# Float16 parts in the experts' products, their weights' norms summed in the first stage, and sigmoids taken for two routing batches at once

## The chip, the cores and the metric

The kernel runs on one core of one Trainium2 chip. The core has five engines with instruction queues of their own: TensorE (PE in the profile; its weight loads are shown apart, as PEld), VectorE (DVE), ScalarE (ACT), GpSimd (POOL) and SyncE (SP, which here only issues DMAs). Each engine works through its queue in order, and semaphores tie the queues together. The metric is the time of one execution on the device, in microseconds (us). Several runs give a median; one further execution is recorded by the profiler, and its times are those of the profile.

## The reference

The input x is 4 sequences of 2048 tokens with 256 channels, 8192 tokens in all. It is normalised over the channels, and two branches are added to it:

```
xn = layernorm(x)
# branch 1: gated linear attention, 8 heads, keys of 128, values of 64
q, k, v = xn @ Wq, xn @ Wk * 128**-0.5, xn @ Wv
alpha = sigmoid((xn @ Wg + bg) / 16)
state[t] = alpha[t] * state[t-1] + outer(k[t], v[t])
attn = (q[t] @ state[t]) * sigmoid(xn @ Wog) @ Wo
# branch 2: mixture of 64 experts, 8 for each token
scores = sigmoid(xn @ gate_w.T)                 # 64 for each token
# groups of 8 experts, the best 4 groups, the best 8 experts in them,
# weights normalised and times 2.5; at most 256 tokens for an expert
y = (silu(rows @ w_gate[e]) * (rows @ w_up[e])) @ w_down[e]
out = x + attn + sum over its experts of weight * y
```

w_gate and w_up are 256x128 for each expert and w_down is 128x256, in float32: 393 KB for an expert and 25.2 MB for all 64.

## The kernel before

**Precision.** Most products are taken from two parts: a value is rounded to a high part, the rest is the low part, and `product` (L267) sums three matmuls: high times high, high times low, low times high. In the attention branch the parts are float16. Since float16 has a small range, a weight is first scaled by a power of two. The power comes from the weight's sum of squares, which ScalarE takes with a Square activation that also accumulates (`squares`, L153), or which TensorE takes (`gram`); two matmuls with the triangular matrices u_le and u_gt add the 128 partitions, and `fit_scales` (L159) makes the power out of the exponent's bits. In the experts' products the parts are of the type float32r, which has float32's range and needs no scaling.

**The attention branch** goes in 32 blocks of 256 tokens (`block`, L1034), and each block in 12 steps. A block projects keys, queries, gates and values (`project`, L810; its matmuls have the lines L269 to L271 and the tile pj). ScalarE takes the high part out of the accumulator and VectorE the low part (`split`, L219: lines L220 and L221, tiles k, qh, ql). The projections share four accumulator banks in the first half of the kernel; a bank is free when both engines have read it.

**The routing** goes in 16 batches of 512 tokens beside the attention of the first 16 blocks. It consists of generators in the list `side`: `front` (L333) normalises a batch and computes its logits, `decays` (L424) makes the decay factors of one to four batches, `back` (L481) selects the experts. Each call of `step()` moves each generator on by one `yield`, from the step number on that stands beside it in `side`. A batch's two sigmoids stand at the end of `front`: sg (L418), for the decays, and sc (L420), for the scores. ScalarE holds the tables of one set of functions; where the next function is not in it, the program has an ACT_TABLE_LOAD. The sigmoid is in another set than the exponential of the attention (L907), and the logarithm of `decays` (L432) in another again.

**The experts** begin with block 16, when `side` is empty: about five for each block, each in five stages at successive turns (`expert_step`, L722). `expert_weights` (L634) loads the three weights into w. `expert_in` (L641) turns the gathered rows (tile xet), and ScalarE takes the high parts wh (L653) and those of the rows (L655); VectorE takes the low part wl one turn later, in `expert_late` (L716, line L719). `expert_mid` (L659) has 12 matmuls into gu, a tanh (L668) and two operations of VectorE that give hs (L669, L671); `expert_split` makes hs into the parts hh and hl. `expert_out` (L681) has six matmuls into yp, and ScalarE multiplies by the routing weight (L691). `expert_add` (L702) adds the rows into the output by an indirect DMA of GpSimd.

**The order of the work.** The program's text gives the dependences, the pools' buffers and some pairs that must follow each other (`tc.issue_after`). A scheduler that simulates the engines then decides how the instructions stand in each engine's queue, and can draw work forward that comes later in the text. The order of the built program can be read without running it. The DMAs of SP stand in one queue, loads for the attention among those for the routing: xs (the block's rows), el, aj and mv (its decays), xt (the next batch), xw_d and xT_d (stores of a batch).

Of the kernel before, what the change touches and what calls it, by code (L numbers as in the profile page):

```python
# [8 lines left out]
F32 = mybir.dt.float32  # L9
F32R = mybir.dt.float32r  # L10
F16 = mybir.dt.float16
# [8 lines left out]
P = 128  # L20
# [25 lines left out]
KFIT = 2.0 ** -11  # L46
VFIT = 2.0 ** -14
FULL = 1024.0
NPART = 3
# [22 lines left out]
def gla_moe_kernel(ctx: ExitStack, tc: tile.TileContext, x, Wq, Wk, Wv, Wo, Wg, bg, Wog,  # L72
# [77 lines left out]
    unfit = const.tile([P, 6], F32, name="unfit")  # L150
    undo = const.tile([P, 1], F32, name="undo")

    def squares(j, t):  # L153
# [125 lines left out]
    r1 = routing.enter_context(tc.tile_pool(name="r1", bufs=1))  # L279
    stg = routing.enter_context(tc.tile_pool(name="stg", bufs=1))  # L280
    stg1 = routing.enter_context(tc.tile_pool(name="stg1", bufs=1))

# [50 lines left out]
    def front(b):  # L333
# [77 lines left out]
        for t in range(RT):  # L411
            for c in range(2):
# [4 lines left out]
                                       op0=ALU.mult, op1=ALU.add)  # L417
        nc.scalar.activation(sg[:, b], zs[:, b], AF.Sigmoid)  # L418
        sc = r3.tile([P, RT, E], F32, name="sc")
        nc.scalar.activation(sc, lg[:, :, 0:E], AF.Sigmoid, scale=unfit[:, GATE:GATE + 1])  # L420
        batch[b]["sc"] = sc
        yield True

# [57 lines left out]
    def back(b):  # L481
# [92 lines left out]
        yield True  # L574

    def lists():
# [56 lines left out]

    def expert_weights(e, m):  # L634
        w = moe["w4"].tile([P, 6, I], F32, name="w", bufs=3)
# [3 lines left out]
        m["w"] = w  # L639

    def expert_in(e, m):  # L641
# [8 lines left out]
        w3, m1 = moe["w3"], moe["m1"]  # L650
        wh = w3.tile([P, 6, I], F32R, name="wh")
        wl = w3.tile([P, 6, I], F32R, name="wl")
        nc.scalar.copy(wh, m["w"])  # L653
        x2 = m1.tile([P, 2, 2, 2, P], F32R, name="xe2")
        nc.scalar.copy(x2, xt)  # L655
        m.update(wh=wh, wl=wl, xh=x2[:, 0], xl=x2[:, 1])
        moe["late"].append((nc.vector, wl, m["w"], wh))

    def expert_mid(e, m):  # L659
# [3 lines left out]
        for k in range(2):  # L663
            for c in range(2):
                product(gu[:, k, :], (wh[:, 2 * k + c, :], wl[:, 2 * k + c, :]),
                        (xh[:, c], xl[:, c]), c == 0, c == 1)
        hs = moe["m1"].tile([P, CAP], F32, name="hs")
        nc.scalar.activation(hs, gu[:, 0, :], AF.Tanh, scale=0.5 / XFIT)  # L668
        nc.vector.scalar_tensor_tensor(hs, in0=hs, scalar=1.0, in1=gu[:, 0, :],  # L669
                                       op0=ALU.add, op1=ALU.mult)  # L670
        nc.vector.tensor_tensor(hs, hs, gu[:, 1, :], ALU.mult)  # L671
        m["hs"] = hs

    def expert_split(e, m):
        hh = moe["m2"].tile([P, CAP], F32R, name="hh")
        hl = moe["m2"].tile([P, CAP], F32R, name="hl")
        nc.scalar.copy(hh, m["hs"])
        moe["late"].append((nc.vector, hl, m["hs"], hh))
        m["h"] = (hh, hl)

    def expert_out(e, m):  # L681
# [8 lines left out]
        for f in range(2):  # L690
            nc.scalar.activation(y[:, f, :], yp[:, f, :], AF.Copy, scale=m["xe"][:, f, D + e:D + e + 1])  # L691
        m["y"] = y
# [23 lines left out]
    def expert_late():  # L716

        for eng, lo, full, hi in moe["late"]:
            eng.tensor_tensor(lo, full, hi, ALU.subtract)  # L719
        moe["late"] = []  # L720
# [481 lines left out]
    def start_front(b):  # L1202
        return 0 if b < 2 else 6 if b == 2 else (b - 2) * STEPS

    for b in range(NB):
        if b:
# [63 lines left out]
```

## Time and profile before

Three runs took 1246.44, 1246.57 and 1249.08 us.

| | us | share of the span |
|---|---|---|
| median of the runs | 1246.57 | |
| profiled execution | 1247.5 | |
| its span, first to last instruction | 1245.6 | 100% |
| TensorE busy | 1191.6 | 96% |
| weight loads busy | 1039.2 | 83% |
| VectorE busy | 967.7 | 78% |
| ScalarE busy | 858.6 | 69% |
| GpSimd busy | 710.5 | 57% |
| ScalarE's table loads, 39 of 1.283 each | 50.0 | 4% |

How to read it: a busy time is a union over the engine's instructions. Matmuls overlap each other and their weight loads, so the duration of one (some 0.28 us) is longer than the distance from one to the next, and the distance is what a matmul costs where TensorE is full. Instructions are grouped as "line engine operation out<-in shape xcount | busy us, mean ns | idle time of the engine just before, and what ended it". The kernel has three stretches: to about 60 us it sets up, to about 590 us the routing runs beside the attention, and from there to about 1195 us the experts do.

### The profile page before, as it was taken

What the parts mean: (1) busy time and instruction counts of PE and PEld (TensorE: products, weight loads), DVE (VectorE), ACT (ScalarE), POOL (GpSimd) and SP (SyncE); (2) the same over time, 40 slices, a digit from 0 to 9 for tenths busy, and PEclk for the clock granted to TensorE, in tenths of its full rate; (3) what the DMA queues carried; (4) which work ended last, traced back from release to release, by engine and by line L of the source; (5) the groups of instructions that cost most, each with busy time, mean ns of one, the idle gap of its engine ahead of it and who ended that gap; (6) DMA issues with size and microseconds to landing.
All of it is one profiled execution on the core that took longest, in us unless ns stands there. A gap on an engine that the chain in (4) does not pass through costs nothing.

```text
span 1245.6 us, 34787 instructions
## 1 busy us (share of the span) xinstructions
PE 1191.6 (96%) x13783; PEld 1039.2 (83%) x13783; DVE 967.7 (78%) x2669; ACT 858.6 (69%) x1536; POOL 710.5 (57%) x899
## 2 busy tenths in 40 slices
PE   6799999989999999999999999999999999999997
PEld 5587788878788788878789899998988898998986
DVE  6987787776777867777978878787878788787764
ACT  5566676666666566665667777777777777777764
POOL 1476577765676576753426665636856567665330
PEclk9999999999999999999999999999999999999999
DMA  7444444333344443322636675767767677766531
GB/s 245 126 129 153 113 130 126 121 96 110 94 128 119 136 128 104 101 67 75 186 101 143 161 174 127 171 149 176 155 157 168 155 160 170 161 143 147 104 68 35
DMA packets 148579, 165.35 MB, mean 133 GB/s; under 512 B 32384, under 2 KB 119296, under 8 KB 147712
## 3 DMA queue, kind: packets, MB, share of 16 engines
q1 hardware_dynamic: 114896, 113.57, 29.4%
q0 software_dynamic: 29712, 45.89, 21.4%
q10 hardware_dynamic: 3808, 3.67, 0.8%
q8 instruction: 108, 1.77, 0.6%
q14 instruction: 55, 0.45, 0.1%
HBM read 115.98 MB, written 58.38 MB: 140 GB/s over the span
## 4 chain that ended last, share of the span: by engine, by line
PE 67%; DVE 14%; ACT 8%; DMA 4%; POOL 4%; issue 2%; SPq 1%; DVEq 0%; ACTq 0%; POOLq 0%
PE pj L269 11%; PE pj L271 11%; PE pj L270 11%; PE od L948 4%; PE od L954 3%; PE kp L887 3%; DMA el<-el_d 3%; PE gu L269 2%; PE gu L271 2%; PE gu L270 2%; PE xet L649 2%; PE sp L269 2%; PE sp L270 2%; PE sp L271 2%; DVE qt L863 2%
## 5 line engine op out<-in xcount | busy, mean ns | idle before, releaser
L705 POOL DMA_INDIRECT out_dram<-y,idx x128 | 212.4, 1659 | 93.4 <-DMA out_dram<-y,idx 24.2
L629 POOL DMA_INDIRECT xe<-xw_d,idx x128 | 133.9, 1046 | 125.9 <-ACT y L691 85.8
L269 PE MATMUL pj<-xs,wq_h 128*128 128x256 f16 x496 | 135.4, 273 | 9.3 <-DVE k L221 8.2
L221 DVE SCALAR_TENSOR_TENSOR k<-pj,k 128x512 f16<-128x512 f32 x128 | 86.9, 685 | 70.4 <-ACT k L220 70.4
L269 PE MATMUL pj<-xs,wk_h 128*128 128x256 f16 x496 | 135.2, 273 | 0.1
L270 PE MATMUL pj<-xs,wq_h 128*128 128x256 f16 x496 | 135.2, 273 | 0.0
L271 PE MATMUL pj<-xs,wk_l 128*128 128x256 f16 x496 | 135.2, 273 | 0.0
L270 PE MATMUL pj<-xs,wk_h 128*128 128x256 f16 x496 | 135.2, 273 | 0.0
L271 PE MATMUL pj<-xs,wq_l 128*128 128x256 f16 x496 | 135.2, 273 | 0.0
L932 DVE TENSOR_TENSOR dc<-sp,dc 128x512 f32<-128x512 f32 x128 | 87.8, 686 | 40.4 <-PE sp L271 26.1
L948 PE MATMUL od<-dc,v 128*64 128x128 f32 x1024 | 102.5, 281 | 6.6 <-DVE dc L932 6.6
L220 ACT ACTIVATE k<-pj 128x512 f16<-128x512 f32 x128 | 74.8, 592 | 43.6 <-PE pj L271 43.2
L270 PE MATMUL sp<-ql,k 128*128 128x128 f16 x512 | 96.1, 219 | 4.2 <-DVE ql L221 3.9
L269 PE MATMUL sp<-qh,k 128*128 128x128 f16 x512 | 99.1, 220 | 0.9 <-ACT qh L220 0.8
L220 ACT ACTIVATE qh<-pj 128x512 f16<-128x512 f32 x128 | 75.9, 596 | 33.0 <-PE pj L271 32.2
L221 DVE SCALAR_TENSOR_TENSOR ql<-pj,qh 128x512 f16<-128x512 f32 x128 | 86.8, 679 | 11.9 <-ACT qh L220 11.7
L271 PE MATMUL sp<-qh,k 128*128 128x128 f16 x512 | 95.9, 219 | 0.0
L954 PE MATMUL od<-qt,state 128*64 128x128 f32 x960 | 94.5, 274 | 0.0
L719 DVE TENSOR_TENSOR wl<-w,wh 128x768 fp32r<-128x768 f32 x64 | 61.2, 956 | 40.5 <-ACT wh L653 37.9
L992 ACT CAST oh<-oT 128x512 fp32r<-128x512 f32 x64 | 39.5, 617 | 74.0 <-DVE oT L962 74.0
L863 DVE SCALAR_TENSOR_TENSOR qt<-pj,el 128x512 f32<-128x512 f32 x128 | 86.9, 679 | 0.0
L906 ACT ACTIVATE dc<-lp 128x512 f32<-128x512 f32 x128 | 76.2, 596 | 13.2 <-PE lp L902 13.2
(408 smaller groups left out, 4539.6 us busy)
## 6 DMA issues: line engine op xcount, KB each, us to landing
el<-el_d SPq DMA_DIRECT2D x64, 512.0 KB
xw_d<-x SPq DMA_DIRECT2D x16, 512.0 KB
xT_d<-xT SPq DMA_DIRECT2D x16, 512.0 KB
out_dram<-in_L_attn_x_dram SPq DMA_DIRECT2D x16, 512.0 KB
w<-in_L_ffn_w_gate_dram SPq DMA_DIRECT2D x64, 128.0 KB
w<-in_L_ffn_w_up_dram SPq DMA_DIRECT2D x64, 128.0 KB
w<-in_L_ffn_w_down_dram SPq DMA_DIRECT2D x64, 128.0 KB
xs<-xT_d SPq DMA_DIRECT2D x31, 256.0 KB
```

Source lines behind the costliest of these rows:

```text
L220: return (nc.scalar.activation(hi, t, AF.Copy, scale=scale).ins, nc.vector.scalar_tensor_tensor(lo, in0=t, scalar=scale, in1=hi, op0=ALU.m ...
L221: nc.vector.scalar_tensor_tensor(lo, in0=t, scalar=scale, in1=hi, op0=ALU.mult, op1=ALU.subtract).ins)
L269: nc.tensor.matmul(out_, lhsT=a[0], rhs=b[0], start=first, stop=False)
L270: nc.tensor.matmul(out_, lhsT=a[0], rhs=b[1], start=False, stop=False)
L271: return nc.tensor.matmul(out_, lhsT=a[1], rhs=b[0], start=False, stop=last).ins
L629: in_turn(lambda: nc.gpsimd.indirect_dma_start(out=xe[:, f, :], out_offset=None, in_=xw_d[:, :], in_offset=bass.IndirectOffsetOnAxis(ap=id ...
L705: two = [in_turn(lambda: nc.gpsimd.indirect_dma_start(out=of, out_offset=bass.IndirectOffsetOnAxis(ap=idx[:, e, f:f + 1], axis=0), in_=m[" ...
L863: read = nc.vector.scalar_tensor_tensor(qt, in0=pj, scalar=QFIT, in1=two_heads(el, i), op0=ALU.mult, op1=ALU.mult)
L906: nc.scalar.activation(dc, lp, AF.Relu, scale=-1.0)
L932: anchor.append(nc.vector.tensor_tensor(dc, B["sp"], dc, ALU.mult).ins)
L948: mm = nc.tensor.matmul(od[i * DV:(i + 1) * DV, n, j, :], lhsT=v[:, h0 + 2 * j + i, :], rhs=dc[:, 2 * j + i, :], start=True, stop=first)
L954: mm = nc.tensor.matmul(od[i * DV:(i + 1) * DV, n, j, :], lhsT=state[half][:, 2 * j + i, :], rhs=qt[:, ck, 2 * j + i, :], start=False, sto ...
```

## The change

Four things are altered.

1. **Types.** wh, wl, the rows' parts, hh and hl become float16. wh is now w times a power of two of the expert's own (`fite`), by an activation with a scale for each partition; wl, and hl likewise, come from a VectorE operation that scales, too. The tanh has the inverse as its scale (`arge`), the product that gives hs is scaled by 2^-44, and the routing weight of an expert's rows is multiplied by what is left over (`rese`), in a new small VectorE operation (`yw`, 128x2).
2. **Norms.** A new generator, `expert_fits`, joins `side` at step 16. It loads each expert's weights into one of three buffers nw and takes the sum of squares with one Square activation over 128x768; after the 64th, two matmuls add the partitions and five VectorE operations make the three scales of all experts. It yields two or three times after each expert.
3. **Loading.** The three DMAs of `expert_weights` move into `load_expert`, which both use. The experts' own loads remain.
4. **Sigmoids.** From batch 2 on, an even batch only has its logits copied into sc by VectorE. The odd batch after it takes sg of both batches in one activation, then the even batch's sc in place, then its own, one behind another.

```diff
+    sqe = const.tile([P, E], F32, name="sqe")
+    fite = const.tile([P, E], F32, name="fite")
+    arge = const.tile([P, E], F32, name="arge")
+    rese = const.tile([P, E], F32, name="rese")
...
+    nw = routing.enter_context(tc.tile_pool(name="nw", bufs=3))
...
-        nc.scalar.activation(sg[:, b], zs[:, b], AF.Sigmoid)
+
         sc = r3.tile([P, RT, E], F32, name="sc")
-        nc.scalar.activation(sc, lg[:, :, 0:E], AF.Sigmoid, scale=unfit[:, GATE:GATE + 1])
         batch[b]["sc"] = sc
+        if b > 1 and b % 2 == 0:
+            nc.vector.tensor_copy(sc, lg[:, :, 0:E])
+        else:
+            b0 = b if b < 2 else b - 1
+            made["sg"] = nc.scalar.activation(sg[:, b0:b + 1].rearrange("p b x y -> p (b x y)"),
+                                              zs[:, b0:b + 1].rearrange("p b x y -> p (b x y)"), AF.Sigmoid).ins
+
+            if b0 < b:
+                with tc.issue_after(made["sg"]):
+                    sc0 = batch[b0]["sc"]
+                    made["sg"] = nc.scalar.activation(sc0, sc0, AF.Sigmoid, scale=unfit[:, GATE:GATE + 1]).ins
+            with tc.issue_after(made["sg"]):
+                nc.scalar.activation(sc, lg[:, :, 0:E], AF.Sigmoid, scale=unfit[:, GATE:GATE + 1])
...
+    def expert_fits():
+
+        last = None
+        for e in range(E + 1):
+            if e < E:
+                w = nw.tile([P, 6, I], F32, name="nw")
+                load_expert(e, w)
+            if last is not None:
+                junk = stg1.tile([P, 6 * I], BF16, tag="junk", name="junk")
+                nc.scalar.activation(junk, last.rearrange("p c i -> p (c i)"), AF.Square,
+                                     accum_out=sqe[:, e - 1:e])
+            last = w
+            for _ in range(2 + e % 2):
+                yield True
+        tot = ps["mo"].tile([P, E], F32, tag="mo", name="tot")
+        for k, u in enumerate((u_le, u_gt)):
+            nc.tensor.matmul(tot, lhsT=u, rhs=sqe, start=(k == 0), stop=(k == 1))
...
-        wh = w3.tile([P, 6, I], F32R, name="wh")
-        wl = w3.tile([P, 6, I], F32R, name="wl")
-        nc.scalar.copy(wh, m["w"])
-        x2 = m1.tile([P, 2, 2, 2, P], F32R, name="xe2")
+        wh = w3.tile([P, 6, I], F16, name="wh")
+        wl = w3.tile([P, 6, I], F16, name="wl")
+        fe = fite[:, e:e + 1]
+        nc.scalar.activation(wh, m["w"], AF.Copy, scale=fe)
+        x2 = m1.tile([P, 2, 2, 2, P], F16, name="xe2")
...
-        nc.scalar.activation(hs, gu[:, 0, :], AF.Tanh, scale=0.5 / XFIT)
+        nc.scalar.activation(hs, gu[:, 0, :], AF.Tanh, scale=arge[:, e:e + 1])
...
-        nc.vector.tensor_tensor(hs, hs, gu[:, 1, :], ALU.mult)
+        nc.vector.scalar_tensor_tensor(hs, in0=hs, scalar=HFIT, in1=gu[:, 1, :], op0=ALU.mult, op1=ALU.mult)
         m["hs"] = hs
+        yw = moe["m2"].tile([P, 2], F32, name="yw")
+        nc.vector.tensor_scalar(yw, m["xe"][:, :, D + e], rese[:, e:e + 1], None, ALU.mult)
...
-            nc.scalar.activation(y[:, f, :], yp[:, f, :], AF.Copy, scale=m["xe"][:, f, D + e:D + e + 1])
+            nc.scalar.activation(y[:, f, :], yp[:, f, :], AF.Copy, scale=m["yw"][:, f:f + 1])
...
-            eng.tensor_tensor(lo, full, hi, ALU.subtract)
+            nc.vector.scalar_tensor_tensor(lo, in0=full, scalar=scale, in1=hi, op0=ALU.mult, op1=ALU.subtract)
...
+    side.append((16, expert_fits()))
```

More of the change, by code (lines that the diff above doesn't have):

```diff
@@ L47 @@
 VFIT = 2.0 ** -14
+HFIT = 2.0 ** -44
 FULL = 1024.0
@@ L574, in back @@
         yield True
+    def expert_fits():
[14 more added lines that the diff above has]
+            nc.tensor.matmul(tot, lhsT=u, rhs=sqe, start=(k == 0), stop=(k == 1))
+        y = stg1.tile([P, E], I32, tag="ye", name="ye")
+        nc.vector.tensor_copy(sqe, tot)
+        nc.vector.tensor_scalar(y, sqe.bitcast(I32), 24, None, ALU.logical_shift_right)
+        nc.vector.tensor_scalar(fite.bitcast(I32), y, -2.0 ** 23, 204 * 2.0 ** 23, ALU.mult, ALU.add)
+        nc.vector.tensor_scalar(arge.bitcast(I32), y, 2.0 ** 23, 39 * 2.0 ** 23, ALU.mult, ALU.add)
+        nc.vector.tensor_scalar(y, y, 20.0, 104.0, ALU.max, ALU.min)
+        nc.vector.tensor_scalar(rese.bitcast(I32), y, 3 * 2.0 ** 23, -60 * 2.0 ** 23, ALU.mult, ALU.add)
+        yield True
     def lists():
@@ L632, in fetch, with load_expert @@
         return dict(xe=xe)
-    def expert_weights(e, m):
-        w = moe["w4"].tile([P, 6, I], F32, name="w", bufs=3)
+    def load_expert(e, w):
         nc.sync.dma_start(out=w[:, 0:2], in_=w_gate[e].rearrange("(c p) i -> p c i", p=P))
@@ L638, in expert_weights @@
         made["w"] = nc.sync.dma_start(out=w[:, 4:6].rearrange("p c i -> p (c i)"), in_=w_down[e]).ins
-        m["w"] = w
+    def expert_weights(e, m):
+        m["w"] = moe["w4"].tile([P, 6, I], F32, name="w", bufs=3)
+        load_expert(e, m["w"])
     def expert_in(e, m):
@@ L650, in expert_in @@
         w3, m1 = moe["w3"], moe["m1"]
-        wh = w3.tile([P, 6, I], F32R, name="wh")
-        wl = w3.tile([P, 6, I], F32R, name="wl")
-        nc.scalar.copy(wh, m["w"])
-        x2 = m1.tile([P, 2, 2, 2, P], F32R, name="xe2")
+        wh = w3.tile([P, 6, I], F16, name="wh")
[3 more added lines that the diff above has]
+        x2 = m1.tile([P, 2, 2, 2, P], F16, name="xe2")
         nc.scalar.copy(x2, xt)
         m.update(wh=wh, wl=wl, xh=x2[:, 0], xl=x2[:, 1])
-        moe["late"].append((nc.vector, wl, m["w"], wh))
+        moe["late"].append((wl, m["w"], fe, wh))
     def expert_mid(e, m):
@@ L667, in expert_mid @@
         hs = moe["m1"].tile([P, CAP], F32, name="hs")
-        nc.scalar.activation(hs, gu[:, 0, :], AF.Tanh, scale=0.5 / XFIT)
+        nc.scalar.activation(hs, gu[:, 0, :], AF.Tanh, scale=arge[:, e:e + 1])
         nc.vector.scalar_tensor_tensor(hs, in0=hs, scalar=1.0, in1=gu[:, 0, :],
                                        op0=ALU.add, op1=ALU.mult)
-        nc.vector.tensor_tensor(hs, hs, gu[:, 1, :], ALU.mult)
+        nc.vector.scalar_tensor_tensor(hs, in0=hs, scalar=HFIT, in1=gu[:, 1, :], op0=ALU.mult, op1=ALU.mult)
         m["hs"] = hs
+        yw = moe["m2"].tile([P, 2], F32, name="yw")
+        nc.vector.tensor_scalar(yw, m["xe"][:, :, D + e], rese[:, e:e + 1], None, ALU.mult)
+        m["yw"] = yw
     def expert_split(e, m):
-        hh = moe["m2"].tile([P, CAP], F32R, name="hh")
-        hl = moe["m2"].tile([P, CAP], F32R, name="hl")
+        hh = moe["m2"].tile([P, CAP], F16, name="hh")
+        hl = moe["m2"].tile([P, CAP], F16, name="hl")
         nc.scalar.copy(hh, m["hs"])
-        moe["late"].append((nc.vector, hl, m["hs"], hh))
+        moe["late"].append((hl, m["hs"], 1.0, hh))
         m["h"] = (hh, hl)
@@ L716, in expert_late @@
     def expert_late():
-        for eng, lo, full, hi in moe["late"]:
-            eng.tensor_tensor(lo, full, hi, ALU.subtract)
+        for lo, full, scale, hi in moe["late"]:
+            nc.vector.scalar_tensor_tensor(lo, in0=full, scalar=scale, in1=hi, op0=ALU.mult, op1=ALU.subtract)
         moe["late"] = []
```

## The prediction

> **What bounds the kernel now.** I read the stages first, then TensorE's rows and waits, then ScalarE's order. Busy time by stage (columns: stage; then for PE, weight loads, DVE, ACT and POOL the busy us and count; granted clock; DMA share; GB/s):
>
> ```profile
> 0.00:20.00 20.00, 9.78 (x79) 9.80 (x79) 13.65 (x57) 6.75 (x14) 5.15 (x25) 1.00 0.85 269
> 20.00:60.00 40.00, 32.26 (x306) 24.59 (x305) 33.75 (x104) 26.04 (x42) 11.46 (x15) 0.96 0.47 154
> 60.00:185.00 125.00, 116.42 (x1406) 99.14 (x1403) 98.91 (x301) 84.59 (x152) 83.37 (x152) 0.97 0.43 130
> 185.00:590.00 405.00, 387.76 (x4669) 327.71 (x4669) 310.51 (x927) 262.06 (x471) 255.83 (x443) 1.00 0.37 107
> 590.00:1180.00 590.00, 586.72 (x6657) 527.65 (x6655) 471.97 (x1208) 444.38 (x801) 340.88 (x255) 1.00 0.67 154
> ```
>
> Experts run from 590 us on; before that is the routing stage. In the expert stage TensorE is busy 586.7 of 590 us, so it sets the time, and only less TensorE work helps. In the routing stage it is busy 93 to 96%; the rest is small waits (waiter, releaser, us, times, longest), from 60 to 590 us:
>
> ```profile
> PE pj L269 <- DVE k L221: 7.2, 8, 1.3
> PE od L948 <- DVE dc L932: 6.3, 5, 2.5
> ```
>
> VectorE's split of k follows ScalarE's copy of k, so both stand for a ScalarE that comes about a microsecond late. How closely the products follow each other shows in the timeline of TensorE (start, us, line, tiles):
>
> ```profile
> 900.05 0.28 PE L269 MATMUL gu<-xe,wh 128*128 128x256 f32 x1
> ...
> 901.35 0.28 PE L271 MATMUL gu<-xe,wl 128*128 128x256 f32 x1
> 901.47 0.28 PE L269 MATMUL pj<-xs,wq_h 128*128 128x256 f16 x1
> ...
> 902.13 0.27 PE L269 MATMUL pj<-xs,wq_h 128*128 128x256 f16 x1
> ```
>
> Eleven steps of gu take 1.30 us, 118 ns each; six of pj, float16 of the same size, 0.66 us, 110 ns. [...]
>
> **1. Float16 products, expert stage.** Each expert has 12 gu and 6 yp products, 1152 in all. Taking each end from the end before it over the whole trace, gu costs 118 ns, yp 127 (it pays some 55 more where it follows a 128-column float16 product), a float16 product of 256 columns 109. So 768 x 118 + 384 x 127 = 139.4 us becomes 1152 x 109 = 125.6: **-13.8 us**. Two products for the norms' sum add 0.5.
>
> Here a rule must be weighed against the rows:
>
> ```profile
> L269 PEld LDWEIGHTS gu<-xe,wh 128*128 128x128 f32 x256 | 48.2, 188 | 0.4 <-issue 0.3
> L269 PEld LDWEIGHTS <-wq_h 128*128 128x128 f16 x512 | 50.1, 98 | 7.7 <-DVE k L221 0.9 <-issue 0.2
> ```
>
> The Trainium skill, "TensorE: Matmul & The Clock Gate", section "Weight-path perf modes — Fast Weight Load (FWL) and DoubleRow", says that the fast weight load is used unless the data are FP32. The rows agree, 188 against 98 ns; priced by that, 1152 x 90 = 104 us would go. But loads overlap products, and the starts above are 118 apart, not 188. I take the 13.8.
>
> ScalarE pays there: wh (a CAST of 836 ns) becomes an ACTIVATE with a scale per partition, and so does the tanh. og, with such a scale, takes 692 ns, qh of the same size without one 596: +96 ns, twice, x64 = 12 us. VectorE gets yw, 128x2, like idx at 158 ns: 10 us; the other VectorE edits swap equals (qt 679, dc 686 ns at one size). ScalarE goes from 444 to 456 of some 577 us (79%), VectorE to 482 (84%), both behind TensorE. Uncovered they would cost 22; I take 0. Stores, gathers and scatters stay.
>
> **2. Squares, routing stage.** 64 experts' weights, 393 KB each, are also read in the first stage: 192 DMAs on SP's queue, 64 Square activations on ScalarE. Nearest rows:
>
> ```profile
> L157 ACT ACTIVATE junk<-wog_f 128x1024 bf16<-128x1024 f32 x1 | 1.1, 1056 | 1.9 <-DMA wog_f<-in_L_attn_Wog_dram 1.9
> L157 ACT ACTIVATE junk<-gate_f 128x128 bf16<-128x128 f32 x1 | 0.3, 310 | 0.0
> L157 ACT ACTIVATION_READ_ACCUMULATOR junk<-gate_f 128x1 f32 x1 | 0.2, 187 | 0.0
> ```
>
> (1056-310)/896 = 0.83 ns an element, so 768 elements take 843 ns, and the read 187, of which 94 overlap: 0.94 us, x64 = 60 us. The text paces the loads over 160 steps, but in the built order they are drawn forward: all 64 Squares stand before the work that in the trace lies at 185 us, 53 of them between 60 and 185. From 20 to 185 us ScalarE was busy 26.0 + 84.6 = 110.6 of 165 us. With the Squares, less four table loads (part 3, 5 us), it needs **166 of 165 us**. Not all of its idle time can be filled: its queue is in order, Squares stand between the copies of k and q that release TensorE's banks, and each may wait for a load. At 92.5% busy, near what the expert stage's engines reach, the stretch takes 179 us: **+14**. Bounds: if Squares only filled holes, +3; if ScalarE can be kept 83% busy (its best 20 us in the trace are 16.4, 82%), 200 us: +35. I take 14, nearer the lower end, because the engine behind it, TensorE, has 16 us idle in that stretch to give.
>
> DMA: queue q1 moved 113.57 MB in 29.4% of 1245.6 us, 310 GB/s at full share; 25.2 MB are 81 us. The stretch had 0.47 x 40 + 0.43 x 125 = 73 us; 154 of 165 would be 93%, of 179, 86%. Only the first 20 us reached 0.85. So the transfers ask for about the same stretch. In SP's order the loads stand in threes between el, xs, lt and aj, so each of these may come some 4 us (three experts at 1.3 us) later; they are fetched about half a block (some 18 us) ahead, which covers that. Each expert's load waits for the Square of the third before it: about 1.4 us of issue, 2.4 us to land (the first w loads, start of wh after the last issue), 0.9 Square, 4.8 us per three buffers against 2.6 us between Squares; it holds on average, not in bursts. Uncovered it is part of the +35.
>
> **3. Sigmoids in pairs.** In the built order ScalarE's table loads fall from 39 to 25, four before 185 us and ten after.
>
> ```profile
> 158.14 1.28 ACT L418 ACT_TABLE_LOAD   x1
> ...
> 163.11 1.28 ACT L907 ACT_TABLE_LOAD   x1
> ```
>
> The Trainium skill, "ScalarE: Activation LUTs", section "What ACT_TABLE_LOAD costs", gives 1283 ns and a drain of about 1380, 2.66 us a switch. The timeline shows the 1283 alone: about 18 ns before and 11 after. So 14 x 1.28 = 18 us of ScalarE, not 37. After 185 us ScalarE is busy 65%, most loads fall into slack; TensorE's idle time within the ten microseconds of such a pair is 1.3 to 2 us against 0.7 as a usual share: about 1 us for each of five pairs, **-5** (by the rule -10; nothing if hidden). VectorE's seven copies of logits, some 0.4 us each, are lost in its 25% of idle time. The deferred sigmoid comes one batch later, still ahead of the routing that reads it.
>
> **Sum.** 1247.5 (the profiled execution: span 1245.6 and 1.9 around it) - 13.3 - 5 + 14 = 1243.2. The runs' median, 1246.57, lies 0.9 lower, within my error; I say **1243**.
>
> **Rivals.**
> - *ScalarE and transfers fill up, slower.* Place: 20 to 185 us. Price: at 83 to 85% ScalarE the stretch grows by 30 to 35, giving 1247.5 - 18.3 + 32 = 1261. It decides once ScalarE stays under 90.5% busy there (166/183: 18 us, all the gain). For it: 93% DMA demand, in-order queues on SP and ScalarE, and TensorE's clock at half for 3.4 us three times before 103 us; longer stalls invite more. Against: TensorE's own slack there.
> - *Squares in holes, faster.* +3 only: 1232. For it: 54 us of ScalarE idle time; against: they aren't where the Squares stand (40 us from 120: 20 Squares, 19 us, for some 13 idle).
> - *Float16 gains nothing*, VectorE or ScalarE then ending last: +13, 1256. Against: 79 and 84% busy.
> - *Weight loads decide after all*, 104 us: 1153. Against: the starts.
>
> **Chances.** Forecast 0.42 (own range 1238 to 1250), holes 0.18, fill-up 0.35, float16 nothing 0.04, weight loads 0.01. 0.2% is 2.5 us, about what a measurement tells from none. The forecast's half below 1244 and the holes make faster 0.44; the strip to 1249 gives same 0.14; slower 0.42. The range runs from 1230 into the fill-up, 1268.
>
> **What would show it.** In the profile after: products gu at 109 ns steps; Squares near 0.84 us; 25 table loads; the work now at 185 us reached near 199, with ScalarE over 90% busy before it; from there to the experts some 5 us less than 405; the expert stage some 13 shorter. If that work comes after 203 us, the sign is wrong; waits of Squares for DMA would name the transfers.

## The result and the profile after

The changed kernel takes **1275.34 us** (median of four runs, 1274.03 to 1278.49) against 1246.51 for the kernel before in the same comparison: a ratio of 1.0231, 95% interval 1.0208 to 1.0254, or 28.8 us slower. The forecast of 1243 had the sign wrong, and the time lies above the range's upper end of 1268 too.

The page of the changed kernel, with its span, the busy time of each engine and the first DMA queue:

```profile
span 1276.8 us, 35276 instructions
PE 1193.0 (93%) x13787; PEld 1022.5 (80%) x13787; DVE 988.7 (77%) x2746; ACT 900.2 (71%) x1643; POOL 716.8 (56%) x899
q1 hardware_dynamic: 158928, 138.75, 35.5%
```

TensorE is as busy as before (1193.0 us, 1191.6 before), although its products became cheaper; its idle time grew from 54.0 to 83.8 us. So the added time is waiting, and the stages tell where. The columns are those of the prediction's table by stage: busy us and count of PE, weight loads, DVE, ACT, POOL; granted clock; DMA share; GB/s. The stretches end at about the same work as in the second table.

```profile
20.00:60.00 40.00, 29.41 (x274) 22.91 (x273) 28.88 (x99) 29.87 (x53) 10.61 (x12) 0.96 0.76 235
60.00:217.00 157.00, 131.42 (x1491) 107.41 (x1489) 106.58 (x320) 123.17 (x257) 85.59 (x157) 0.96 0.82 244
217.00:496.00 279.00, 262.54 (x3150) 221.60 (x3148) 216.28 (x641) 172.41 (x317) 181.02 (x321) 0.99 0.39 115
496.00:637.00 141.00, 132.55 (x1543) 111.95 (x1541) 106.05 (x299) 84.00 (x150) 76.11 (x122) 0.99 0.33 91
637.00:1210.00 573.00, 565.93 (x6560) 496.08 (x6560) 475.96 (x1253) 445.35 (x787) 344.90 (x254) 1.00 0.67 155
```

The kernel before, in the stretches with the work of the last three:

```profile
189.00:465.00 276.00, 262.55 (x3171) 221.80 (x3169) 212.27 (x638) 182.35 (x329) 181.94 (x325) 1.00 0.40 118
465.00:598.00 133.00, 128.08 (x1514) 108.12 (x1512) 101.63 (x290) 81.31 (x145) 74.02 (x118) 1.00 0.33 92
598.00:1180.00 582.00, 579.84 (x6592) 522.19 (x6590) 465.11 (x1194) 440.05 (x793) 340.24 (x254) 1.00 0.67 154
```

The work that began at 189 us begins at 217: 28 us are lost before it. Another 3 go in the next 279 us, 8 between 496 and 637 us, where no Square is left, and the experts give some 8 back (9 by these stretches, of which the last ends a good microsecond off; 7.9 by the marks below). In the first stage TensorE is busy 84% (131.42 of 157), and ScalarE 78% (123.17), not the 90 the prediction wanted to see.

For finer reading I use one mark in each block of 256 tokens: the start of its first product of decays and scores on VectorE (tile dc, L932 before, L985 after). The trace of a second execution of the kernel before, on another occasion, has every mark within 1.1 us of the first, most within 0.4; two traces of the changed kernel differ by up to 2.2. A mark tells where time is lost, but it is one execution: that of `pairs_tied` took 1270.38 us, the longest of its four (1261.97 to 1270.38), and that of `copy_alone` 1256.25 (median of ten 1253.74). What a kernel costs is read from the ratio of the times.

The table gives these shifts against the kernel before, at the start of blocks 5, 11, 16 (the first with experts) and 31 (the last), and the ratio of the times.

The runs in the lower half were made on two other chips, on which the kernel before itself takes 1273.8 and 1273.6 us; their ratios stand beside their own chip's kernel before, and of their marks only those of the routing stage are used. No trace of the kernel before was taken there, but the kernels run there lose their further time in the experts' stage: `loads_wall` is 15.9 us late at block 16, 40.8 at block 31, and 15.6 in the time against its own chip's kernel before. Those with float16 end far better by their ratio than by block 16 (`no_pairs` 36.2 us late there, 15.6 at the end), so on these chips the change of types seems to give back more, by an estimate from block 16 and the times 16 to 21 us, not 8. What a part costs in the routing is therefore read at block 16, and a ratio from these chips isn't set beside one from the others.

| run | block 5 | 11 | 16 | 31 | ratio (95%) |
|---|---|---|---|---|---|
| `before_again` | -0.4 | -0.1 | +0.1 | +0.4 | |
| changed kernel | +31.0 | +28.5 | +39.1 | +31.2 | 1.0231 (1.0208 to 1.0254) |
| `after_again` | +29.4 | +28.2 | +38.6 | +30.6 | 1.0234 (1.0206 to 1.0262) |
| `f16_alone` | -0.1 | +0.1 | +1.0 | -6.9 | 0.9936 (0.9917 to 0.9954) |
| `f16_plain` | -2.0 | -1.4 | +0.1 | -13.1 | 0.9893 (0.9868 to 0.9918) |
| `pairs_alone` | +6.6 | +7.2 | +15.4 | +15.2 | 1.0104 (1.0086 to 1.0122) |
| `copy_alone` | +0.9 | -0.1 | +7.1 | +7.5 | 1.0036 (1.0022 to 1.0050) |
| `pairs_tied` | +4.6 | +14.3 | +22.4 | +22.4 | 1.0118 (1.0087 to 1.0149) |
| `x_tied` | +3.7 | +7.0 | +10.4 | +10.5 | 1.0087 (1.0062 to 1.0113) |
| `norms_alone` | +32.3 | +35.0 | +35.7 | +36.0 | 1.0282 (1.0249 to 1.0315) |
| `norms_loads` | +24.3 | +25.5 | +27.5 | +27.7 | 1.0196 (1.0168 to 1.0224) |
| `norms_squares` | +7.8 | +8.8 | +10.8 | +10.9 | 1.0081 (1.0063 to 1.0100) |
| `norms_paced` | +12.9 | +30.5 | +38.6 | +38.2 | 1.0306 (1.0288 to 1.0324) |
| other chips: | | | | | |
| `f16_no_norms` | +3.5 | +4.4 | +14.6 | | 0.9966 (0.9949 to 0.9984) |
| `loads_alone` | +20.2 | +18.2 | +27.1 | | 1.0093 (1.0059 to 1.0128) |
| `squares_alone` | +14.3 | +14.2 | +24.0 | | 1.0036 (1.0015 to 1.0057) |
| `paced` | +11.7 | +21.3 | +26.0 | | 1.0063 (1.0042 to 1.0085) |
| `no_pairs` | +32.4 | +34.8 | +36.2 | | 1.0121 (1.0065 to 1.0178) |
| `loads_wall` | +3.2 | +10.6 | +15.9 | | 1.0117 (1.0057 to 1.0175) |

### The profile page after: what moved, and what is told of

Same layout as the page of the kernel before. It is cut to its first block, busy times and chain, and to the rows that moved or that the text cites. A ratio compares the mean times of both kernels' runs of the same rounds, so it can differ in the third digit from the quotient of the medians.

```text
span 1276.8 us, 35276 instructions
## 1 busy us (share of the span) xinstructions
PE 1193.0 (93%) x13787; PEld 1022.5 (80%) x13787; DVE 988.7 (77%) x2746; ACT 900.2 (71%) x1643; POOL 716.8 (56%) x899
## 4 chain that ended last, share of the span: by engine, by line
PE 55%; DVE 13%; DMA 9%; POOL 9%; ACT 8%; issue 3%; SPq 2%; ACTq 0%; POOLq 0%; DVEq 0%
PE pj L276 9%; PE pj L278 9%; PE pj L277 9%; PE od L1001 3%; DMA nw<-in_L_ffn_w_down_dram 3%; PE od L1007 3%; DMA el<-el_d 2%; PE kp L940 2%; PE gu L276 2%; PE xet L698 2%; PE gu L277 2%; PE gu L278 2%; PE sp L277 1%; DVE ql L228 1%; PE sp L276 1%
## 5 line engine op out<-in xcount | busy, mean ns | idle before, releaser
L676 POOL DMA_INDIRECT xe<-xw_d,idx x128 | 139.0, 1086 | 40.3 <-issue 29.0
L985 DVE TENSOR_TENSOR dc<-sp,dc 128x512 f32<-128x512 f32 x128 | 87.7, 685 | 47.3 <-POOL dc L965 23.6
L276 PE MATMUL sp<-qh,k 128*128 128x128 f16 x512 | 100.0, 221 | 14.2 <-ACT qh L227 6.3
L227 ACT ACTIVATE k<-pj 128x512 f16<-128x512 f32 x128 | 75.1, 592 | 39.8 <-PE pj L278 39.1
L940 PE MATMUL kp<-identh,k 128*128 128x128 f16 x1024 | 82.6, 222 | 3.7 <-ACT res L1058 1.6
L960 ACT ACTIVATE dc<-dc 128x512 f32<-128x512 f32 x128 | 81.0, 633 | 2.1
```

Of the source, the lines that this page charges most:

```text
L227: return (nc.scalar.activation(hi, t, AF.Copy, scale=scale).ins, nc.vector.scalar_tensor_tensor(lo, in0=t, scalar=scale, in1=hi, op0=ALU.m ...
L276: nc.tensor.matmul(out_, lhsT=a[0], rhs=b[0], start=first, stop=False)
L676: in_turn(lambda: nc.gpsimd.indirect_dma_start(out=xe[:, f, :], out_offset=None, in_=xw_d[:, :], in_offset=bass.IndirectOffsetOnAxis(ap=id ...
L940: nc.tensor.transpose(kp[:, i, :], k[:, i, :], identh)
L985: anchor.append(nc.vector.tensor_tensor(dc, B["sp"], dc, ALU.mult).ins)
```

## The experiments

### The changed kernel with the norms' halves taken out

`f16_no_norms` is the changed kernel without the norms' loads and Squares:

```diff
-                w = nw.tile([P, 6, I], F32, name="nw")
-                load_expert(e, w)
+                w = None
...
-                junk = stg1.tile([P, 6 * I], BF16, tag="junk", name="junk")
-                nc.scalar.activation(junk, last.rearrange("p c i -> p (c i)"), AF.Square,
-                                     accum_out=sqe[:, e - 1:e])
+                pass
```

`sqe` is set to 4.0 once. `loads_alone` keeps the loads, `squares_alone` keeps the Squares on one resident tile, and `paced` keeps both and ties the loads behind `made["el"]` and the Squares behind the newest exponential of the decays.

> The changed kernel without the 64 Squares and their loads; the sums of squares are a constant (4.0 for each partition, about what these weights give), so the scales no longer follow the data. Theory of the norms: all that the change loses comes from them, so without them its gains stand alone: about 1229 us (13 of float16, 5 of the sigmoids), work that lies at 189.5 us before within 2 us of it, an expert stage some 13 us shorter. Rival of the order: the new order of the queues, the sigmoids in triples above all, loses time by itself also after 217 us; then 1240 or more, with half-clock stretches after 400 us as in the changed kernel.

> The changed kernel with the 192 early loads and without the 64 Squares (constant sums). Theory of the transfers in contention (el, xs and the decays come late behind the loads): 20 us or more above the kernel without norms. Theory of ScalarE's time, and that of the Squares waiting for their loads: within 5 us of it, since nothing waits for these loads any more but the buffers.

> The changed kernel with the 64 Squares on one tile that is there from the start, and without their loads. Theory of ScalarE's time: 60 us of Squares still fill it, 14 to 25 us above the kernel without norms, though not the whole 45. Theory of Squares that wait for their loads, with ScalarE's queue behind them: under 8 us above it, because the scheduler then puts Squares into idle time only.

> The changed kernel with each expert's loads tied behind the latest el load on SP's queue and each Square behind the latest decay's exponential on ScalarE's, so that both spread over the whole routing stage instead of its first 217 us. Theory of concentration (ScalarE and DMA are over-full only together and only there): at most 12 us above the kernel without norms, 1232 to 1242. Rival, that each Square costs the chain about its time wherever it stands: 64 x 0.7 us or more, so no better than the changed kernel, 1270 to 1280.

Without the norms the first stage's loss is nearly gone (block 5: +3.5, where the changed kernel has +31). The loads bring back 16.7 there and the Squares 10.8; together that is 27.5, the 31 less 3.5. So the two halves add up there, and the loads are the larger. Both lie between what was expected of either theory (20 or more, or under 5, for the loads; 14 to 25, or under 8, for the Squares). But from block 11 to 16 all four lose another 5 to 10 us, even with no norm at all: the rival of the order is right in part. Pacing the norms left 11.4 us of their cost at block 16 (26.0 less 14.6), where in the changed kernel they cost 24.5 (39.1 less 14.6); by the times it is 12.0 above `f16_no_norms`, as the theory of concentration said.

### Each part alone, on the kernel before

`pairs_alone` is the kernel before with the changed kernel's sigmoids; `f16_alone` the kernel before with float16 parts, scales for each partition from a constant `sqe`, and `yw`, but without pairs or norms. Two more runs repeat the two kernels.

> The kernel before with the sigmoids of two batches taken one behind another, and nothing else. Theory of saved table loads: 3 to 7 us faster (0.994 to 0.998). Theory of the order: the new order of ScalarE's queue brings the stall of the transposes on ScalarE's rounding of x after 430 us (3 us, then half clock), as in the changed kernel and in the one without norms, and loses 5 to 10 us (1.004 to 1.008).

> Float16 parts with constant sums of squares, no norms, and the sigmoids batch by batch as before. Theory of float16's shorter steps: an expert stage 13 us shorter and nothing lost ahead of it, 0.987 to 0.991. Rival, that the gain is given back in stalls or in the clock while TensorE has less to do: 0.995 or more, with an expert stage of the same length.

> The kernel before, unchanged, for a trace from the same chip as the kernels beside it: its blocks are what theirs are compared with. If the chip alone makes the difference between the two levels of time seen so far (1246 and 1274 us), the lost time shows in it as stalls of TensorE or half-clock stretches that the first trace doesn't have.

> The changed kernel, unchanged, beside the kernel before on this chip. Theory of the norms: slower by 2 to 2.6% as at first, with the loss in its first 217 us. Rival, that the level of the chip decides more than the change: a ratio within 1% of 1.

The pairs, taken alone, lose 13 to 15 us (by the ratio and by the mark), more than either expectation, although 14 table loads are gone. One of the places is at 201 us. ScalarE of `pairs_alone` (start, us, line, operation, tiles, form):

```profile
198.86 0.59 ACT L917 ACTIVATE dc<-lp 128x512 f32<-128x512 f32 x1
199.35 2.06 ACT L386 ACTIVATE xt<-xt,nb,rstd 128x256 f32<-128x256 f32 x4
201.44 1.28 ACT L918 ACT_TABLE_LOAD   x1
202.73 0.63 ACT L918 ACTIVATE dc<-dc 128x512 f32<-128x512 f32 x1
203.26 0.58 ACT L220 ACTIVATE k<-pj 128x512 f16<-128x512 f32 x1
203.74 1.13 ACT L390 CAST x<-xt 128x512 f16<-128x512 f32 x2
```

The same stretch of ScalarE in `before_again`:

```profile
195.09 0.59 ACT L906 ACTIVATE dc<-lp 128x512 f32<-128x512 f32 x1
195.70 1.28 ACT L907 ACT_TABLE_LOAD   x1
196.99 0.63 ACT L907 ACTIVATE dc<-dc 128x512 f32<-128x512 f32 x1
197.53 1.06 ACT L220 ACTIVATE k<-pj 128x512 f16<-128x512 f32 x2
```

And what TensorE of `pairs_alone` waits for there (in brackets the idle time and what ended it):

```profile
201.19 0.27 PE L271 MATMUL pj<-xs,wq_l 128*128 128x256 f16 x1
204.41 0.29 PE L330 MATMUL tp<-identh,x 128*128 128x128 f16 x2 [2.94 <-ACT x L390]
```

Before, the four activations of the next batch's rows (xt, 2.06 us) come after the exponential and both k. With the pairs the scheduler puts them ahead, and it puts the turning of those rows (tp) into TensorE's queue between two projections. The rounding that tp needs (L390) now stands behind 4.9 us of other work, and TensorE, in order, waits. This stall and a like one of 3.0 us at 487 us are 6 of the 15; the rest lies in smaller waits. The table load there is the one of the exponential, which both kernels have. Nothing in the pairs' text asks for this order; it is how the simulated order falls out.

Is it the order, or the later sigmoid? `copy_alone` takes only the copy of the logits by VectorE, and keeps a sigmoid for each batch, with 39 table loads. `pairs_tied` keeps the pairs and ties the xt activations behind the exponential. `x_tied` is this tie alone on the kernel before:

```diff
-        nc.scalar.activation(sc, lg[:, :, 0:E], AF.Sigmoid, scale=unfit[:, GATE:GATE + 1])
+        nc.vector.tensor_copy(sc, lg[:, :, 0:E])
+        nc.scalar.activation(sc, sc, AF.Sigmoid, scale=unfit[:, GATE:GATE + 1])
```

```diff
+                    with tc.issue_after(made["dc"]):
                         nc.scalar.activation(xt[:, t, :], xt[:, t, :], AF.Identity,
```

> The kernel before with one edit: each batch's logits are copied by VectorE and the sigmoid is taken from the copy; each batch still has its own, so the table loads stay 39. If the burst of the pair is what costs: within 0.2% of 1 (0.998 to 1.002). If any new order of the routing's queues can cost several us: 1.004 or more. If the copy itself holds VectorE: 16 x 0.4 us, at most 1.005.

> The sigmoids in pairs as in pairs_alone, and the four activations that normalise x tied behind the latest decay's exponential on ScalarE's queue, so that they no longer stand between the sigmoids and the exponential's table load. Theory of the order: pairs_alone lost by that place; with it undone 1.000 or less, with no stall of 3 us of the transposes on ScalarE's rounding near 204 and 487 us. Rival, the burst (three sigmoids and a table load in a row hold up the copies of k and q): still 1.006 to 1.012.

> The kernel before with one edit: the activations that normalise x are tied behind the latest decay's exponential; 39 table loads, no pairs. pairs_tied was 7 us above pairs_alone. Theory that the tie itself costs that: 5 to 9 us (1.004 to 1.007). Theory that the tie is harmless and the triple of sigmoids is what costs in both: within 2.5 us (0.998 to 1.002).

`copy_alone` saves no table load and defers nothing, and still loses 4.5 us by its ratio. Its traced execution loses 7, nearly all after block 12, above all in two stalls of 2.8 and 2.6 us (tp waiting for L390, at 478 and 514 us); so most of it isn't VectorE's time for the copies, the third expectation. A loss a third to a half as large as that of the pairs comes with no deferral at all. My idea that one place decides fell with `pairs_tied`: the tp stall is gone, but waits of up to 2.0 us for VectorE's ql came in its place, 16.4 us in all from 60 to 600 us (1.5 before). It loses 14.7 by its ratio (22 in its traced execution, the longest of four), which is no less than `pairs_alone`, and not more either beyond the intervals. The tie by itself costs 10, a little above what was expected. What is shown: four small edits of ScalarE's routing work, with the same arithmetic, cost 4 to 15 us each by their ratios. Why the order before is better than each of these isn't shown, and no run has the pairs in the old order.

### What the norms' loads wait for, and who waits for them

`norms_alone` is the kernel before plus the generator with its loads and Squares, whose results nothing reads. `norms_loads` and `norms_squares` are its halves (loads without Squares; Squares on a resident tile), and `norms_paced` has the ties of `paced`. `no_pairs` is the changed kernel with a sigmoid for each batch.

> The kernel before with the 64 Squares and their loads, whose results nothing uses. By the blocks of the traces so far (after less pairs) 22 to 26 us, all before the fifth block: 1.017 to 1.021. Rival, that norms and pairs only lose together because both fill ScalarE: 1.010 or less.

> The kernel before with the 192 early loads and no Squares, float32r and the sigmoids batch by batch. The norms alone cost 35 us. Theory of two halves that add: 12 to 20 us (1.010 to 1.016), with a long stall behind a late el load on GpSimd's queue. Rival, that the Squares and their wait for the loads are all of it: under 5 us (1.004).

> The kernel before with the 64 Squares on a tile that is there from the start and no early loads. Theory of two halves that add: 8 to 15 us (1.006 to 1.012), in many stalls of about 1 us. Rival, that only Squares which wait for a load hurt: under 5 us (1.004). If this and the loads' kernel together stay 8 us or more below 35, the rest is the wait of the one for the other.

> The kernel before with the norms, each expert's loads tied behind the latest el load and each Square behind the latest decay's exponential, so that both spread over the routing stage. Theory of concentration: 8 to 16 us in place of 35 (1.006 to 1.013), spread over the sixteen blocks. Rival, that the work costs the same wherever it lies: 28 us or more (1.022).

> The changed kernel with the sigmoids batch by batch again: float16 and norms alone. If the parts add (norms 35.6 less float16 7.4): 1276 us, a ratio near 1.022, no better than the changed kernel. If the pairs' 15 us stand beside the norms in full: 1260, near 1.011.

The norms alone cost 35.7 us at block 16, against 39.1 for the whole change. Their halves cost 27.5 and 10.8, 38 together, so here, too, they add up; the loads cost more than the 20 us expected at most. `no_pairs` has +36.2, `norms_alone` +35.7 and the changed kernel +39.1: beside the norms the pairs cost some 3 us, not 15. (The ratio of `no_pairs`, 1.0121, looks like the other expectation, but it comes from a chip on which float16 gives back more.) Pacing cost as much here (38.6) as no pacing, where it had helped by 13 us in the changed kernel. The ties may cost by themselves, as in `x_tied`, so whether loads and Squares come too thickly stays undecided.

Why do loads that nothing reads cost 27 us? SP's queue of `norms_loads`, from 82 us:

```profile
82.33 0.43 SPq L666 DMA_DIRECT2D nw<-in_L_ffn_w_gate_dram  x1
...
83.88 0.38 SPq L475 DMA_DIRECT2D el_d<-els  x1
84.31 1.14 SPq L666 DMA_DIRECT2D nw<-in_L_ffn_w_gate_dram  x1
85.50 0.47 SPq L667 DMA_DIRECT2D nw<-in_L_ffn_w_up_dram  x1
87.09 0.37 SPq L840 DMA_DIRECT2D el<-el_d  x1
```

And that of the kernel before:

```profile
79.06 0.32 SPq L469 DMA_DIRECT2D el_d<-els  x1
80.46 0.89 SPq L807 DMA_DIRECT2D el<-el_d  x2
```

el (the block's decays) is read back from memory, and in the kernel before each read is issued only 3.6 to 5.4 us before its first reader: here 80.46, and GpSimd's copy wall<-el at 85.39; in the next blocks 101.2 and 105.3, 118.3 and 121.9, 138.8 and 144.2. In `norms_loads` this el has 87.09 and 91.55, 4.5 us. Here the transfer isn't slower (at the five reads from 109.8 us on wall comes 5.0 to 7.7 us after the issue, so there it may be); it starts 6.6 us later. Of these, 3.3 were lost before (the mark of block 1); the other 3.3 come from SP's queue, where store and read stand among loads that take SP half a microsecond each. Summing SP's DMA instructions from 20 us to the start of block 4, the kernel before issues 78 of them in 39.7 us of 170, `norms_loads` 264 in 136.9 us of 190, the changed kernel 264 in 137.5 of 197. What follows the late el, on GpSimd:

```profile
91.55 0.19 POOL L902 COPY wall<-el 128x8 f32<-128x8 f32 x1 [6.09 <-DMA el<-el_d]
91.71 0.20 POOL L372 TENSOR_TENSOR nt<-nt,va 128x4 f32<-128x4 f32 x1
...
94.94 0.22 POOL L376 TENSOR_SCALAR nb<-nb 128x4 f32<-128x4 f32 x1
```

on ScalarE:

```profile
95.20 2.07 ACT L392 ACTIVATE xt<-xt,nb,rstd 128x256 f32<-128x256 f32 x4 [8.34 <-POOL nb L376]
97.18 0.60 ACT L1025 CAST oh<-oT 128x512 fp32r<-128x512 f32 x1
97.68 0.59 ACT L939 ACTIVATE dc<-lp 128x512 f32<-128x512 f32 x1
```

and on TensorE:

```profile
98.32 0.37 PE L274 MATMUL pj<-xs,wq_h 128*128 128x256 f16 x1 [4.80 <-ACT dc L939]
```

GpSimd stands before wall, 8 numbers to a partition. Behind wall is the inverse root of the next batch's variance (nt to nb), which ScalarE's xt activation needs; behind that are oh and dc in ScalarE's queue, and dc frees a bank of TensorE. The mark of block 2 is 10.4 us late: 3.3 us of a late read have become 7. Over the stretch from 60 us on these are the two waits that grew most (waiter, releaser: us, times, longest). `norms_loads`, 60 to 217 us:

```profile
POOL wall L902 <- DMA el<-el_d: 28.2, 7, 6.1
ACT xt L392 <- POOL nb L376: 15.2, 4, 8.3
```

`before_again`, from 60 us to the same work at 200, had `wall` waiting 7.4 us for el and `xt` 2.1 us for nb. wall is not the reader that el is fetched for. In the kernel before, VectorE's product with the el of 80.46 (counting loads and products in order) comes 36 us after the issue, and those of the next four loads 47 to 54 us after it; the order of GpSimd's queue just puts the small copy where el lands.

```profile
116.31 0.68 DVE L863 SCALAR_TENSOR_TENSOR qt<-pj,el 128x512 f32<-128x512 f32 x1
```

To test the chain, `loads_wall` moves the copy from GpSimd to VectorE, behind that product, and leaves the loads:

```diff
-                B["aux"].tensor_copy(wall, el[:, :, :, P - 1])
+                nc.vector.tensor_copy(wall, el[:, :, :, P - 1])
```

> The early loads without Squares as in norms_loads, and the small copy wall, which waits for el, moved from GpSimd's queue to VectorE's behind the product that reads el anyway. Theory of the chain (late el holds wall, wall holds GpSimd's queue, so the batch's normalising comes late, so ScalarE's queue stands): the stalls of 5 us go, 1.004 to 1.012. Rival, that el's lateness itself or the shared bandwidth costs the 27 us: 1.017 or more.

The loss at block 5 falls from 24.3 to 3.2 us, on a chip that is slower, not faster; the ratio, 1.0117, lies within what the theory of the chain said. The same el is issued at 89.77 us, no earlier, and wall comes 30 us later:

```profile
89.77 0.38 SPq L840 DMA_DIRECT2D el<-el_d  x1
119.64 0.15 DVE L902 COPY wall<-el 128x8 f32<-128x8 f32 x1
```

The DMA share is no smaller (0.82 in `norms_loads` from 60 to 213.8 us):

```profile
60.00:215.00 155.00, 146.36 (x1797) 124.48 (x1795) 124.98 (x384) 105.74 (x191) 102.22 (x179) 1.00 0.88 259
```

At 88% of the DMA engines' time TensorE is busy 94%. So in this stage neither the amount of the transfers nor SP's issues (132 us of 171 here) made most of the loss of `norms_loads`, but GpSimd's in-order wait for a late el. (The move gives a new order, too; that one of its own saves 21 us here is unlikely beside the 28.2 us of waits that went, but not excluded.) After block 5 `loads_wall` loses 13 more, in stalls like those of the pairs (2.8 us of tp for ScalarE at 379); it is no cure for the whole time, and was not tried on the changed kernel.

The changed kernel, which has the Squares as well, is hardly slowed by this chain. There wall waits little more than before (5.4 us at the same work), and xt has no wait for nb, as in `norms_alone` (7.5 us and none); `loads_alone`, without Squares, has 23.4 and 17.7. From 60 to 217 us:

```profile
POOL wall L922 <- DMA el<-el_d: 9.9, 6, 3.8
```

Its late loads show at another door. The chain of waits from 20 us to about the start of block 5, summed by line:

```profile
by line: DMA nw<-in_L_ffn_w_down_dram 17.6%; ACT junk L605 6.7%; issue 6.6%; DMA xt<-in_L_attn_x_dram 4.4%; DMA nw<-in_L_ffn_w_gate_dram 3.5%; DMA xT_d<-xT 3.2%; DMA el_d<-els 2.7%; DVE dc L985 2.6%; SPq L683 2.4%; ACT k L227 2.3%; DMA el<-
```

The same of the kernel before, from 20 to 189 us:

```profile
by line: DMA el<-el_d 7.4%; PE pj L269 5.2%; PE pj L271 5.0%; PE pj L270 5.0%; issue 3.4%; DVE qt L863 2.8%; DVE st L340 2.8%; DVE dc L932 2.7%; DVE ql L221 2.5%; DMA gbias<-in_L_ffn_gate_bias_dram 2.4%; ACT L907 2.3%; PE od L948 2.3%; PE k
```

Before, el heads the chain and TensorE's projections follow. After, Squares and what they wait for head it, and no projection is among the lines shown. What ScalarE and SP wait for in the changed kernel from 20 to 217 us:

```profile
ACT junk L605 <- DMA nw<-in_L_ffn_w_down_dram: 19.7, 15, 3.6
...
SPq L682 <- ACT junk L605: 17.4, 15, 2.9
```

Fifteen Squares hold ScalarE's queue for a load, up to 3.6 us each, with the exponentials and the copies of k and q behind them; fifteen times the next load holds SP's queue for a Square to free one of three buffers, with el behind it. That these waits are what the norms cost in the changed kernel is read from its trace; no run takes them away and keeps both loads and Squares at their places.

### The experts' stage, and a faster kernel

The experts' stage of `before_again`, `f16_alone` and the changed kernel's repeat (`after_again`), by windows:

```profile
598.50:1185.70 587.20, 584.93 (x6635) 526.40 (x6634) 466.37 (x1198) 442.50 (x798) 344.17 (x256) 1.00 0.67 153
```

```profile
599.40:1178.80 579.40, 572.68 (x6626) 501.63 (x6627) 481.35 (x1265) 449.54 (x795) 347.45 (x256) 1.00 0.67 154
```

```profile
636.90:1216.30 579.40, 572.68 (x6627) 501.56 (x6628) 480.88 (x1265) 449.45 (x795) 348.52 (x256) 1.00 0.67 154
```

With float16 TensorE is busy 12.2 us less, near the 13.3 forecast, but the stage is 7.8 shorter: 4.4 us came back as idle time (2.3 to 6.7). `f16_alone` (0.9936, between its two expectations) gains the same with no norms and no pairs, so what is lost here has nothing to do with them. VectorE has 15 us more work. The suspects were the activations with a scale for each partition, and yw. `f16_plain` takes fixed powers of two in their place:

```diff
+HFIT = 2.0 ** -44
+WFIT = 2.0 ** 9
...
-        nc.scalar.copy(wh, m["w"])
+        nc.scalar.activation(wh, m["w"], AF.Copy, scale=WFIT)
...
-        nc.scalar.activation(hs, gu[:, 0, :], AF.Tanh, scale=0.5 / XFIT)
+        nc.scalar.activation(hs, gu[:, 0, :], AF.Tanh, scale=0.5 / (XFIT * WFIT))
```

Its parts are float16, and wsum takes the factor that yw had. The scale is set for weights of this size and doesn't follow the data, as the changed kernel's does.

> Float16 parts with fixed powers of two as immediates: no norms, no pairs, no scale for each partition, no small product yw; the scales don't follow the data. Theory that float16's gain is cut by the 96 ns more of two activations and by yw: the stalls from 640 to 930 us go, 0.989 to 0.991. Rival, that they come from the order and TensorE's being nearer the other engines: as f16_alone, 0.993 to 0.995.

`f16_plain` takes 1235.33 us (1234.36 to 1235.86; 1248.23 before): 12.9 us faster than the kernel before on the same chip, and faster than `f16_alone` by 5.0. By block 31 its gain is 13.1. The operation that makes wh (min/median/max in ns), in `f16_alone`:

```profile
L689 ACT ACTIVATE wh<-w,fite x64: 930/936/994, 591.6 to 1164.4; 128x768 f16<-128x768 f32 x64
```

and in `f16_plain`:

```profile
L661 ACT ACTIVATE wh<-w x64: 840/843/870, 590.1 to 1154.6; 128x768 f16<-128x768 f32 x64
```

A scale from a tile costs 93 ns, a constant nearly none (the CAST of `before_again` took 832). The two versions differ in these activations (wh, and the tanh with 474 against 383), in wl (1017 ns, 956 with the constant) and in yw (228 ns, none with the constant), and by 5 to 6 us. TensorE's idle time in the same stage is 4.1 us, 2.6 less than in `f16_alone`. Which of the four takes how much was not separated, nor whether the new order that such an edit brings has a part in it.

## Why the prediction was wrong

**1. Float16 products: the mechanism right, its cover wrong.** The price of a product was right: 109 to 110 ns a step after, and TensorE's busy time fell by 12.2 us for the 13.3 forecast. The weight loads' 90 ns, weighed and set aside, indeed brought nothing. The failed term is "Uncovered they would cost 22; I take 0": with that work, `f16_alone` is 5 to 6 us slower than `f16_plain` without it (a new order may have a part in it). The work was also larger than supposed: yw takes 228 ns, not 158, and wl 61 more, not the same. VectorE at 83% over the stage is not VectorE free at the moment when TensorE needs its k or ql.

**2. Norms: the largest error.** Forecast +14, measured +35.7 alone. Two steps failed.

The loads: "they are fetched about half a block (some 18 us) ahead, which covers that" is the step that failed by most. It holds for the product that el is fetched for (36 to 54 us ahead, more than supposed), but not for el's first reader, the copy wall, 4.9 us behind the issue. The trace of before could have told, for its 32 copies on GpSimd had 24.2 us of idle time in front of them, put down to el:

```profile
L869 POOL COPY wall<-el 128x8 f32<-128x8 f32 x32 | 8.6, 269 | 25.1 <-DMA el<-el_d 24.2 <-PE od L954 0.7
```

The delay was as small as the 4 us supposed (3.3 at the place shown), but with nothing to cover it, it passed through three queues and grew to 7. `norms_loads` measures the term that was put at nothing: 27.5 us; in the changed kernel's own series the loads are 16.7 at block 5. With the Squares in, the loads were covered no better, but by the traces it was Squares that waited for them ("holds on average, not in bursts", 19.7 us on the last of three loads), not wall. (Without the loads' cost the sum of the other parts would still be above nothing, some +7 with the pairs at 3.)

The second is "At 92.5% busy" as a rule for the stretch. ScalarE never got there (78%): it waited in order for loads while it had work behind. The Squares' price was right, 0.84 and 0.19 us, and `norms_squares` gives 10.8 for the 14 forecast. So this term was about right in size, but as the price of Squares alone; that it comes so near is in part luck, since the 92.5% it rests on did not come about.

The rival named the place and the transfers, and put the sum at +32. Its point of decision, a ScalarE under 90.5% busy, came true, but read as a limit of capacity, not as waits in order.

**3. Sigmoids in pairs: wrong in sign.** The count was right, 25 table loads for 39. Forecast -5, measured +13 to 15 alone and some 3 beside the norms. The failed step is "about 1 us for each of five pairs": it took the order around the loads as given. That order changed, and each stall of tp it brought (2.9 and 3.0 us) is longer than a load that went (1.28). No run has fewer loads in the old order, so the price of a load, by the row or by the rule, was never tested.

**The sum.** Alone, the parts give +15.2 + 36.0 - 6.9 = +44; together they give +31. I had added parts as if each met the kernel before, and had no term at all for a new order.

**What stays open.** Why the pairs cost little beside the norms; how much of the 8 us lost between blocks 12 and 16 is order and how much the sigmoids' one batch of delay; which of the waits around the Squares make the changed kernel's loss, since the chain that was tested is that of the loads alone; and why two of the chips take 26 us more and give back more with float16.

## What to carry to other kernels

A load that nobody waits for still delays the loads behind it in its queue: before adding one, read for each neighbour the time from issue to its first reader, not only to the main one, and look for small in-order instructions that already wait for it, for what is behind them waits too. If nobody needs such an instruction yet, move it behind the main reader: here that took 21 of 24 us off the first five blocks, and 12 of 27 off the whole stage. Where a scheduler orders the queues, an edit of a shared stage also buys a new order, here worth 4 to 15 us against a gain of 5 in the sum: make a neutral edit of the same place and measure it. And a gain in the engine that sets the time may be given back by the operations added beside it: here the version with a constant scale and no extra product kept 5 to 6 us more than the one with scales from a tile.

## What the runs showed of the hardware

After a stall of one to three microseconds TensorE's granted clock can halve (0.5 in the records), deep in the run too. In the changed kernel, at 688 us:

```profile
687.75 0.57 PE L276 MATMUL pj<-wo_h,oh 128*128 128x256 f32 x1 [1.18 <-ACT kt L945]
688.12 0.42 PE L277 MATMUL pj<-wo_l,oh 128*128 128x256 f32 x1
688.34 0.42 PE L278 MATMUL pj<-wo_h,ol 128*128 128x256 f32 x1
```

These products follow each other every 0.21 to 0.22 us, where the step of such a product is otherwise 0.118. The records show such stretches of 3.4 us three times in the kernel before, at 41, 65 and 99 us, and eight times in the changed one (and once at the very end of each), the last three at 476, 510 and 688 us, behind waits of 2.06, 3.03 and 1.18 us. The Trainium skill, "TensorE: Matmul & The Clock Gate", section "What's actually happening", puts an idle window of about 3.4 us ahead of the slow clock; the length of the slow stretches agrees with that figure, but the waits in front of these were shorter, and not every wait of this length is followed by one (the 2.94 us of `pairs_alone` at 204 us is not). At half speed each costs up to 1.7 us on top of the stall that preceded it, so the five more are up to 8.5 of the 28.8 us. `f16_alone` has one at 650 us.

The same kernel took 1247.7 to 1248.8 us on two chips and 1273.6 to 1273.8 on two others, 2% apart, as much as the change itself. Two executions of the kernel before had every mark within 1.1 us of each other and the last within 0.4, so its waits are close to the same each time; the edited kernels vary more (6 us over ten runs of `copy_alone`, 8 over four of `pairs_tied`).
